# A modulated two-layer block on one core: the first modulation loaded and used in smaller parts, and some VectorE steps hung elsewhere

## The chip, the core and the metric

The kernel runs on one core of a Trainium2 chip. The engines of a core run side by side, each with its own queue of instructions that it takes in order: TensorE (PE in the profile, with its weight loads as PEld), VectorE (DVE), ScalarE (ACT), GpSimd (POOL) and SyncE (SP), whose queue here issues most of the transfers. The metric is the device time of one execution in microseconds. Before the change three runs took 585.10, 585.11 and 585.63 us, a median of 585.11.

## The reference, cut to what matters

The input x has 2 batches of 2048 tokens of width 512, everything in float32. A row of 512 numbers per batch (cond) gives six rows of modulation.

```
emb = silu(cond) @ ada_w + ada_b                      # ada_w is 512 x 3072
shift1, scale1, gate1, shift2, scale2, gate2 = split(emb, 6)
n  = ln(x) * (1 + scale1) + shift1
x  = x + gate1 * (gelu_erf(n @ w1 + b1) @ w2 + b2)     # 512 -> 512 -> 512
n  = ln(x) * (1 + scale2) + shift2
x  = x + gate2 * (gelu_tanh(n @ fw1 + fb1) @ fw2 + fb2) # 512 -> 1024 -> 512
```

`ln` takes mean and variance over the 512 columns of a token.

## The kernel before, in words

The 4096 tokens are cut into 8 blocks of 512 (`xs[i]`, i = 0 to 7; four blocks are one batch). A block is held as four slots c of 128 tokens. For each block the kernel makes n1 (the first normalised input, class `Norm`, which 1), hA (the first hidden layer, class `First`), the residual oA, n2 (`Norm`, which 2), hC (the second hidden layer, class `Second`) and the residual oC. The order of all this is written out by hand, block 0 and 1 first, then a loop over i = 1 to 7 in which the stages of neighbouring blocks are interleaved.

A matrix product is done with seven half-size products instead of eight, P1 to P7 in the code. Their operands are sums of quarters of the matrices: `sums_of_first` and `sums_of_second` (L350 in the profile) write them, for weights on POOL, for activations on DVE or POOL. A quarter of an activation is half of the columns of width (chunks k = 0, 1 or k = 2, 3 of 128) by half of the tokens of the block (slots c = 0, 1 or c = 2, 3). P1 of hA reads the first tokens of k = 0 and 1, P2 those of k = 2 and 3. Each product is accumulated in PSUM banks called y, x and v, read by DVE or ACT (L747, L757, L764, L767 for hidden layers, L802 for residuals), and the next product into the same bank waits for that read. The products of hC from block 1 on come from a table of 26 products, each of 128 x 256 twice (`products`, L1130 for the matmuls, L1147 for the reads on DVE, L1144 for those on ACT).

`hooks` is the means by which other work is put between products: `hook(hooks, places, ops)` hangs small pieces at named products, and each piece is issued just after the product and its read. An engine's own order follows from that, so a piece on DVE stands between two reads of products.

The start is this. SP issues the loads in order: x_0 in two halves, two slabs of ada_w (`load_ada`, 512 x 512 each: g = 0 for shift1, g = 1 for scale1), w1, x_1, the slab g = 2 (gate1), eight-descriptor pieces of ada_b for the gate, w2, b2, and so on. There are eight semaphores for transfers, used in turn by ACT's and SP's queues together, so the issue of a transfer waits for the one eight places before it. PE runs matmuls on a unit matrix (`warm`, tile `idle`) until data is there. The vectors cond, ada_b, b1 and fb1 come in on ACT's queue and are turned by PE (tile `rowsT`) into columns (`colsT`). `modulation(0, part)` makes 16 matmuls of 32 output rows over four chunks of the contraction (L276, tile `pada`), a transpose of 128 x 128 on DVE (L293) and an addition (L297). Block 0 is normalised on ACT and DVE (L627, L631), turned by PE (L656, 16 transposes, chunk by chunk over the four slots), and scaled and shifted by `modulate` on ACT (L676) and DVE (L678) from PSUM, one instruction of 128 x 512 for each k. Then hA_0 begins (`py_hA`, L496). Inside hA_0 stand the statistics of x_1 on ACT (L545, L556), the gate rows (L276, L305), the spread of the gate to all partitions (L312, `pgate`, which needs the 0/1 matrix `picks`), and the multiplication of w2 by the gate (`fold`, L398).

Three places further on matter here. In the residual of block 1 and the first group of hC_0 the eight row chunks of fw2 are multiplied by gate2, one DVE instruction of 128 x 512 each (`fold5`, L398). For the second batch the gates are folded again, and with them the biases: `gate_bias` loads b2 or fb2 and its `multiply` multiplies the row by the gate on DVE (L1030) and takes the first half from the second (`apart_row`, L479). For b2 this hangs at step 8 of the 26 products of hC_3 (`late_bias`), for fb2 at the last product of hA_5.

Of the kernel before, what the change touches and what calls it, by code (L numbers as in the profile page):

```python
# [36 lines left out]
F32 = mybir.dt.float32  # L37
# [103 lines left out]
def kernel(  # L141
# [65 lines left out]
    def load_ada(g):  # L207
        ada[g] = big_tile(f"ada_{g}")
        nc.sync.dma_start(
            out=ada[g], in_=ada_w[:, g * D : (g + 1) * D].rearrange("(k p) n -> p k n", p=P)  # L210
        )

    def load_w(name, w, t=None, eng=nc.sync):
        if t is None:
            t = const.tile([P, w.shape[0] // P, w.shape[1]], F32, tag=name, name=name)
        eng.dma_start(out=t, in_=w.rearrange("(k p) n -> p k n", p=P))
        return t
# [22 lines left out]
    ident = w2_t[:, :P]  # L240
    make_identity(nc, ident)
    load_x(0, 2)
    load_ada(0)
    load_ada(1)
    w1_sb = load_w("w1", w1)
    load_x(1)
    load_ada(2)

# [35 lines left out]
                )  # L284
        return pa

    def modulation(g0, part, pa=None):

        g = g0 + part
        if pa is None:  # L290
            pa = rows_of(g)
        turned = pa[:, P : 2 * P]
        nc.vector.transpose(turned, pa[:, :P])  # L293
# [3 lines left out]
        nc.vector.tensor_tensor(m, turned[:, :, :B], bias.unsqueeze(2).to_broadcast([P, KD, B]), ALU.add)  # L297
        mods[g0, part] = m
# [178 lines left out]
    def apart_row(row, eng):  # L477

        eng.tensor_tensor(row[:, D // 2 :], row[:, D // 2 :], row[:, : D // 2], ALU.subtract)  # L479
# [40 lines left out]
    class Norm:  # L520
# [57 lines left out]
        def rest(self, scratch=None):  # L578
# [11 lines left out]
            v.tensor_tensor(self.nmr, self.mv[:, :, 0], self.rstd, ALU.mult)  # L590
            v.tensor_scalar(self.nmr, self.nmr, -1.0, None, ALU.mult)

        def steps(self, scratch=None):
# [58 lines left out]
        def transpose(self, k, pt=None):  # L652
            if pt is None:
                pt = ps_t.tile([P, TB], F32, tag="t", name=f"pt{self.name}_{k}")
            for c in range(C):
                nc.tensor.matmul(  # L656
                    pt[:, c * P : (c + 1) * P],
                    self.xn[:, c, k * P : (k + 1) * P],
                    ident,
                    start=(c == 0),  # L660
                    stop=(c == C - 1),
                    is_transpose=True,
                    skip_group_check=True,
                )
            return pt

        def modulate(self, k, pt=None, eng=None):
# [3 lines left out]
            dst = self.nT.rearrange("p a (k c q) -> p a k c q", k=KD, c=C)[:, :, k]  # L671
            src = dst if pt is None else pt.rearrange("p (c a q) -> p a c q", c=C, a=C)
            if pt is None:
                dst = src = self.nT[:, :, k * P : (k + 1) * P]
            if eng is None:
                nc.scalar.activation(dst, src, AF.Identity, bias=shift, scale=scale)  # L676
            else:
                eng.tensor_scalar(dst, src, scale, shift, ALU.mult, ALU.add)  # L678

        def turned(self, on_dve=()):  # L680

            return [
                lambda k=k: self.modulate(k, self.transpose(k), nc.vector if k in on_dve else None)
                for k in range(KD)
            ]

        def moved(self, engs=(None,)):

# [337 lines left out]
    def gate_bias(g, b, row, name):  # L1026

        t = load_row(work.tile([P, D], F32, tag=f"gb{g}", name=name, bufs=1), row)
        def multiply():
            nc.vector.tensor_tensor(t, gate[g, b], t, ALU.mult)  # L1030
            apart_row(t, nc.vector)

        return t, multiply

# [182 lines left out]
    b1T = colsT[:, R_B1:R_FB1]  # L1217
    fb1T = colsT[:, R_FB1:ROWS]

    idle = ps_g.tile([P, C, P], F32, tag="v", name="idle")  # L1220
    def warm(count, blocks=2):
        for _ in range(count):
            nc.tensor.matmul(
# [10 lines left out]
    warm(1, 1)  # L1234

    run(n1[0].stats())
    nc.vector.tensor_copy(colsT, pt[:, :ROWS])


    nc.scalar.activation(  # L1240
# [2 lines left out]
        AF.Silu,  # L1243
    )

    for g in (1, 4):
        rows_g = colsT[:, R_ADA + g * KD : R_ADA + (g + 1) * KD]
        nc.vector.tensor_scalar(rows_g, rows_g, 1.0, None, ALU.add)

    picks = brows[:, 3].rearrange("p (m q) -> p m q", m=P // G)  # L1250
# [3 lines left out]
    n1[0].scales()  # L1254

    w1_ops, w1_sums, _ = weight_of_first("w1", w1_sb)
    run(w1_sums)
    modulation(0, 0)
    warm(3)
    for c in range(C):  # L1260
        n1[0].normal(c, nc.vector if c % 2 else None, on_pe=True)
    modulation(0, 1)
    pts = {}

    def transposed(k):
        pts[k] = n1[0].transpose(k, ps_g.tile([P, TB], F32, tag="yv"[k % 2], name=f"pt1_0_{k}"))

    for k in range(KD):
        transposed(k)
    for k in range(KD):  # L1270
        n1[0].modulate(k, pts[k], nc.vector if k % 2 else None)
# [159 lines left out]
    for i in range(1, NBLK):  # L1431
# [167 lines left out]
        hooks = {}  # L1599
        hook(hooks, ("P1",), [begin])  # L1600
        if refold5:
            hook(hooks, ("P4",), [multiply_5])
            hook(hooks, ("P5",) * 6 + ("P7", "P7", "P3"), folds)
        if refold2:
            def bias_2():
                take_gate(2, b)
                gb[2], multiply_2 = gate_bias(2, b, b2, f"gb2_{b}")
                return multiply_2
# [63 lines left out]
```

## Time and profile before

| | us |
|---|---|
| median of three runs | 585.11 |
| the profiled execution | 585.16 |
| its span in the profile | 583.3 |
| PE busy | 575.7 |
| DVE busy | 442.7 |
| POOL busy | 416.5 |
| ACT busy | 284.4 |

Between the span and the time of the profiled execution lie 1.86 us that no engine's rows show. The timeline view gives for each row the start and the length in us from the start of the span, the engine, the line, the operation, output and inputs, shapes and count; brackets at the end hold the idle time of the engine before the row and what ended it. The PE rows hold two passes per matmul instruction, so 4 instructions show as x8.

### The profile page before, as it was taken

How to read it: one execution, taken by the hardware profiler on the slowest of the kernel's cores; microseconds unless marked ns; L12 is line 12 of the kernel's file. 1: busy time of each engine (PE TensorE's matmuls, PEld its weight loads, DVE VectorE, ACT ScalarE, POOL GpSimd, SP SyncE). 2: the span in 40 equal slices, each digit the busy share in tenths (PEclk: the TensorE clock that was granted, in tenths of full speed). 3: DMA queues.
4: the chain of work that ended last, by engine and by line, in shares of the span. 5: the costliest groups of instructions: out<-in, count | busy, mean ns of one | idle time of the engine just before them, and what ended most of it. 6: DMA issues, size and time to landing. Idle time of an engine off the chain costs nothing.

```text
span 583.3 us, 9818 instructions
## 1 busy us (share of the span) xinstructions
PE 575.7 (99%) x3359; PEld 514.4 (88%) x3359; DVE 442.7 (76%) x893; ACT 284.4 (49%) x546; POOL 416.5 (71%) x446
## 2 busy tenths in 40 slices
PE   8999999999999999999999999999999999999997
PEld 4888888888899889998899988998888998899896
DVE  4877888896878576796967678986766487787676
ACT  2828357805652655545634588326664331732520
POOL 1575449999949788599968999998770593369351
PEclk9999999999999999999999999999999999999999
DMA  8977423302205303353033820243130330031002
GB/s 320 391 212 257 105 69 83 103 37 108 60 15 144 145 1 73 119 174 105 2 92 72 305 76 22 51 106 133 52 73 0 98 120 1 1 74 74 0 1 73
DMA packets 26014, 57.57 MB, mean 99 GB/s; under 512 B 4928, under 2 KB 5996, under 8 KB 24300
## 3 DMA queue, kind: packets, MB, share of 16 engines
q1 hardware_dynamic: 22240, 52.20, 28.3%
q10 hardware_dynamic: 3724, 4.75, 3.3%
q8 instruction: 27, 0.44, 0.3%
q14 instruction: 23, 0.19, 0.1%
HBM read 32.80 MB, written 8.40 MB: 71 GB/s over the span
## 4 chain that ended last, share of the span: by engine, by line
PE 88%; DVE 4%; DMA 2%; POOL 2%; ACT 1%; SPq 1%; issue 1%; ACTq 0%; DVEq 0%; POOLq 0%
PE px_hC L1130 10%; PE py_hA L496 8%; PE py_oC L904 8%; PE pv_hC L1130 8%; PE py_hC L1130 8%; PE pl_oC_P_y L952 8%; PE pl_oC_P_v L952 5%; PE pv_hA L496 4%; PE py_oA L839 4%; PE py_oA L496 3%; PE pl_oC_P_x L952 3%; PE py_oC L496 2%; PE py_hC L496 2%; PE px_hA L496 2%; PE pv_oC L952 2%; PE pl_oA_y L854 2%
## 5 line engine op out<-in xcount | busy, mean ns | idle before, releaser
L576 POOL TENSOR_TENSOR r<-ve,minus_half 128x4 f32<-128x4 f32 x16 | 16.6, 1039 | 71.7 <-DVE pl_oC_P_v L604 33.8
L676 ACT ACTIVATE nT<-nT,mod,mod 128x512 f32<-128x512 f32 x34 | 24.9, 804 | 67.8 <-DVE x L966 25.8
L1054 POOL TENSOR_TENSOR forms<-forms 128x256 f32<-128x256 f32 x56 | 42.5, 759 | 4.8 <-DVE forms L1050 1.3
L1130 PE MATMUL py_hC<-forms,fw 128*128 128x256 f32 x168 | 41.4, 381 | 0.4 <-DVE hClo L1147 0.4
L350 POOL TENSOR_TENSOR hSC<-hClo,hChi 128x512 f32<-128x512 f32 (+1 forms) x16 | 19.0, 1193 | 26.5 <-ACT hChi L1125 22.9
L1147 DVE TENSOR_TENSOR hClo<-hClo,py_hC 128x512 f32<-128x512 f32 x42 | 28.5, 683 | 11.1 <-ACT hClo L1144 8.7
L1130 PEld LDWEIGHTS py_hC<-forms,fw 128*128 128x128 f32 x168 | 31.6, 190 | 5.7 <-DVE hClo L1147 1.4
L533 DVE BATCH_NORM_STATS2 st<-x 128x6 f32<-128x512 f32 x48 | 32.4, 676 | 4.9 <-DMA x<-in_x_dram 4.9
L676 ACT ACTIVATE x<-x,mod,mod 128x512 f32<-128x512 f32 x24 | 17.6, 802 | 34.6 <-DMA x<-blocks 25.4
L627 ACT ACTIVATE nT<-x,nmr,rstd 128x512 f32<-128x512 f32 x36 | 26.8, 804 | 7.5 <-DVE nmr L612 4.9
L638 DVE STREAM_TRANSPOSE blocks<-nT 128x512 f32<-128x512 f32 x36 | 25.0, 704 | 5.9 <-ACT nT L627 5.9
L1147 DVE TENSOR_TENSOR hChi<-hChi,pv_hC 128x512 f32<-128x512 f32 x35 | 23.2, 680 | 8.0 <-PE pv_hC L1130 5.4
L1125 ACT ACTIVATE hClo<-hClo,colsT 128x256 f32<-128x256 f32 x56 | 25.3, 499 | 5.6 <-DVE hClo L1147 5.4
L1130 PE MATMUL px_hC<-forms,fw 128*128 128x256 f32 x112 | 27.6, 379 | 0.0
L966 DVE TENSOR_TENSOR x<-pl_oC_P_y,x 128x256 f32<-128x256 f32 (+1 forms) x66 | 24.6, 374 | 1.9 <-PE pl_oC_P_y L952 0.6
L1125 ACT ACTIVATE hChi<-hChi,colsT 128x256 f32<-128x256 f32 x56 | 25.1, 496 | 1.9 <-DVE hChi L1147 1.9
L1144 ACT ACTIVATE hClo<-px_hC 128x512 f32<-128x512 f32 x21 | 12.5, 596 | 27.6 <-PE px_hC L1130 19.3
L904 PE MATMUL py_oC<-fw_s,hSC 128*128 128x256 f32 x112 | 25.3, 379 | 0.0
L904 PE MATMUL py_oC<-fw,hClo 128*128 128x256 f32 x112 | 25.3, 379 | 0.0
L350 POOL TENSOR_TENSOR hClo<-hClo 128x512 f32<-128x512 f32 (+1 forms) x23 | 24.4, 1063 | 0.0
L1144 ACT ACTIVATE hChi<-py_hC 128x512 f32<-128x512 f32 x14 | 7.6, 594 | 34.4 <-PE py_hC L1130 25.5
L1130 PEld LDWEIGHTS px_hC<-forms,fw 128*128 128x128 f32 x112 | 21.3, 190 | 2.9
(403 smaller groups left out, 1850.8 us busy)
## 6 DMA issues: line engine op xcount, KB each, us to landing
x<-in_x_dram SPq DMA_DIRECT2D x13, 1024.0 KB
out_dram<-x SPq DMA_DIRECT2D x14, 512.0 KB
ada<-in_L_cond_ada_w_dram SPq DMA_DIRECT2D x6, 1024.0 KB
x<-blocks SPq DMA_DIRECT2D x96, 64.0 KB
nT<-blocks SPq DMA_DIRECT2D x88, 64.0 KB
fw<-in_L_cond_ff_w_dram SPq DMA_DIRECT2D x2, 2048.0 KB
nT<-blocks ACTq DMA_DIRECT2D x56, 64.0 KB
w<-in_L_cond_ssm_w_dram SPq DMA_DIRECT2D x3, 1024.0 KB
```

The lines of the kernel that those rows point to most:

```text
L350: eng.tensor_tensor(out[:, r], a[:, r], b[:, r], f)
L496: nc.tensor.matmul(ps[b][j * apart][:, j, :], lhs(p, j, k), rhs(p, j, k), start=(fresh and j * (not apart) == 0 and k == 0), stop=(p in (" ...
L533: nc.vector.bn_stats(st, xs[self.i][:, c, :])
L627: nc.scalar.activation(t, x_c, AF.Identity, bias=self.nmr[:, c : c + 1], scale=self.rstd[:, c : c + 1])
L638: nc.vector.transpose(self.bl[:, :, :, c, :].rearrange("p m k q -> p k m q"), self.nT[:, c, :].rearrange("p (k m q) -> p k m q", k=KD, m=C),)
L676: nc.scalar.activation(dst, src, AF.Identity, bias=shift, scale=scale)
L904: yield lambda j=j, k=k: nc.tensor.matmul(ps[BANK[p]][:, j, :], hops(p, j, k), wops[p][:, k, :], start=False, stop=(k == kdim - 1), skip_g ...
L952: nc.tensor.matmul(t[:, n, :], hops.leaves[p][f][:, k, :], leaf_wops[p][f][:, k, :], start=room not in started, stop=(f in ("P2", "P3", "P ...
L1054: eng.tensor_tensor(reg[d], reg[a], reg[b], ALU.add if f == "+" else ALU.subtract)
L1125: nc.scalar.activation(h, h, AF.Gelu_apprx_tanh, bias=fb1T[:, m : m + 1])
L1130: nc.tensor.matmul(ps[b][:, j, :], fa[ra][:, j * P : (j + 1) * P], fb[rb].rearrange("p a (c q) -> p c a q", q=Q), start=(fresh and j == 0) ...
L1147: nc.vector.tensor_tensor(dest(d), dest(d), ps[b], op)
```

## The change: what it does

- The slabs of shift1 and scale1 are loaded together by parts of the contraction: chunks k = 0 and 1 (1 MB), then k = 2, then k = 3 (0.5 MB each), in rows of 4 KB. w1 is loaded in two halves of its rows. SP so issues two more transfers ahead of x_1.
- `rows_01` makes the matmuls of both parts chunk by chunk into one PSUM tile, and `modulation_01` turns and adds both at once (128 x 256). Two of the three `warm` matmuls between them are gone.
- `colsT` is copied by ACT instead of DVE; `picks` is copied by POOL behind the sums of w1 instead of by DVE; `first_steps` needs one small DVE instruction fewer than `steps`.
- The 16 transposes of block 0 go slot by slot: slot 1 ahead of the matmuls of k = 3, slots 0, 3 and 2 behind them.
- `modulate` of block 0 has two instructions of 128 x 256 for each k, first tokens first.
- Of the eight `fold5` pieces the third moves from the last product of oA_1 to P6 of hC_0, and the later ones move so that two hang at P5.
- `gate_bias.multiply` becomes three instructions of 128 x 256, which leave the first product of the second half in the gate's PSUM tile; for b2 they hang at steps 5, 8 and 12 of hC_3 instead of both at 8; for fb2 they stay at the last product of hA_5.

```diff
-    load_ada(0)
-    load_ada(1)
-    w1_sb = load_w("w1", w1)
+    ada_01 = [big_tile(f"ada_{h}").rearrange("p (k g) n -> p k (g n)", g=2) for h in range(2)]
+    def load_ada_01(ks):
+        nc.sync.dma_start(
+            out=ada_01[ks[0] // 2][:, ks[0] % 2 : ks[-1] % 2 + 1],
+            in_=ada_w[ks[0] * P : (ks[-1] + 1) * P, : 2 * D].rearrange("(k p) n -> p k n", p=P),
+        )
+    load_ada_01((0, 1))
+    load_ada_01((2,))
+    load_ada_01((3,))
+    w1_sb = const.tile([P, KD, D], F32, tag="w1", name="w1")
+    load_half("w1", w1, w1_sb, 0)
+    load_half("w1", w1, w1_sb, 1)
...
+    def rows_01(pa, ks):
+        for k in ks:
+            w = ada_01[k // 2][:, k % 2].rearrange("p (g n m q) -> p g m n q", g=2, n=KD, q=G)
+            for g in range(2):
+                for m in range(P // G):
+                    nc.tensor.matmul(
+                        pa[m * G : (m + 1) * G, g * P : (g + 1) * P],
+                        silu[:, k, :],
+                        w[:, g, m],
...
+    def modulation_01(pa):
+        turned = pa[:, 2 * P : 4 * P]
+        nc.vector.transpose(turned, pa[:, : 2 * P])
+        turned = turned.rearrange("p (g n q) -> p g n q", g=2, n=KD)
+        m = const.tile([P, 2, KD, B], F32, tag="mod_0", name="mod_0")
+        bias = colsT[:, R_ADA : R_ADA + 2 * KD].rearrange("p (g n) -> p g n", g=2)
+        nc.vector.tensor_tensor(m, turned[:, :, :, :B], bias.unsqueeze(3).to_broadcast([P, 2, KD, B]), ALU.add)
...
+            else:
+                part = slice(h * C // 2, (h + 1) * C // 2)
+                dst = self.nT.rearrange("p a (k c q) -> p a k c q", k=KD, c=C)[:, :, k, part]
+                src = pt.rearrange("p (c a q) -> p a c q", c=C, a=C)[:, :, part]
...
         def multiply():
-            nc.vector.tensor_tensor(t, gate[g, b], t, ALU.mult)
-            apart_row(t, nc.vector)
+            pg, lo, hi = gate[g, b], slice(0, D // 2), slice(D // 2, D)
+            return [
+                lambda: nc.vector.tensor_tensor(t[:, lo], pg[:, lo], t[:, lo], ALU.mult),
+                lambda: nc.vector.tensor_tensor(pg[:, hi], pg[:, hi], t[:, hi], ALU.mult),
+                lambda: nc.vector.tensor_tensor(t[:, hi], pg[:, hi], t[:, lo], ALU.subtract),
+            ]
...
-    nc.vector.tensor_copy(colsT, pt[:, :ROWS])
+    n1[0].root()
+    nc.scalar.copy(colsT, pt[:, :ROWS])
...
+    n1[0].first_steps()
+    w1_ops, w1_sums, _ = weight_of_first("w1", w1_sb)
+    run(w1_sums)
+    pada_01 = ps_t.tile([P, D], F32, tag="t", name="pada_01")
+    rows_01(pada_01, (0, 1))
+    warm(1)
+    for c in range(C):
+        n1[0].normal(c, nc.vector if c % 2 else None, on_pe=True)
     for g in (1, 4):
...
-    modulation(0, 0)
-    warm(3)
-    for c in range(C):
-        n1[0].normal(c, nc.vector if c % 2 else None, on_pe=True)
-    modulation(0, 1)
...
+    rows_01(pada_01, (2,))
+    n1[0].transpose(1, pts, True)
+    rows_01(pada_01, (3,))
+    for c in (0, 3, 2):
+        n1[0].transpose(c, pts, False)
+    modulation_01(pada_01)
+    for h in range(2):
+        for k in range(KD):
+            n1[0].modulate(k, pts[k], nc.vector if k % 2 else None, h)
...
-    nc.vector.tensor_copy(
+    nc.gpsimd.tensor_copy(
         picks, ident.rearrange("p (m q) -> p m q", q=G)[:, :, :1].to_broadcast([P, P // G, P])
...
-    hook(hooks, ("P7", "P3", "P4"), fold5(0, 3))
+    hook(hooks, ("P7", "P3"), fold5(0, 2))
...
-    hook(hooks, ("P6", "P5", "P7", "P3", "P4"), fold5(3, 8))
+    hook(hooks, ("P6", "P5", "P5", "P7", "P3", "P4"), fold5(2, 8))
...
-            hook(hooks, (8,), late_bias)
+            hook(hooks, (5, 8, 12), late_bias)
...
-            hook(hooks, ("P4",), [multiply_5])
+            hook(hooks, ("P4",), multiply_5())
...
-            late_bias = [lambda: found["gb2"]()]
+            late_bias = [lambda n=n: found["gb2"][n]() for n in range(3)]
```

More of the change, by code (lines that the diff above doesn't have):

```diff
@@ L285, in rows_of, with modulation @@
         return pa
-    def modulation(g0, part, pa=None):
+    def rows_01(pa, ks):
[7 more added lines that the diff above has]
+                        w[:, g, m],
+                        start=(k == 0 and g == 0),
+                        stop=(k == KD - 1),
+                        tile_position=(0, m * G),
+                        skip_group_check=True,
+                    )
+    def modulation_01(pa):
[5 more added lines that the diff above has]
+        nc.vector.tensor_tensor(m, turned[:, :, :, :B], bias.unsqueeze(3).to_broadcast([P, 2, KD, B]), ALU.add)
+        for part in range(2):
+            mods[0, part] = m[:, part]
+    def modulation(g0, part, pa):
         g = g0 + part
-        if pa is None:
-            pa = rows_of(g)
         turned = pa[:, P : 2 * P]
@@ L591, in rest, with first_steps @@
             v.tensor_scalar(self.nmr, self.nmr, -1.0, None, ALU.mult)
+        def first_steps(self):
+            n, v = self.name, nc.vector
+            self.rstd, self.nmr = [small.tile([P, C], F32, tag=t, name=f"{t}{n}") for t in ("rstd", "nmr")]
+            room = ps_t.tile([P, D], F32, tag="t", name=f"small{n}")
+            a, b = room[:, :C], room[:, C : 2 * C]
+            v.tensor_scalar(a, self.mv[:, :, 1], EPS, None, ALU.add)
+            v.tensor_tensor(b, self.r, a, ALU.mult)
+            v.scalar_tensor_tensor(b, b, -0.5, self.r, ALU.mult, ALU.mult)
+            v.scalar_tensor_tensor(self.rstd, b, 1.5, self.r, ALU.add, ALU.mult)
+            v.scalar_tensor_tensor(self.nmr, self.mv[:, :, 0], -1.0, self.rstd, ALU.mult, ALU.mult)
         def steps(self, scratch=None):
@@ L650, in move, with transpose @@
                     )
-        def transpose(self, k, pt=None):
-            if pt is None:
-                pt = ps_t.tile([P, TB], F32, tag="t", name=f"pt{self.name}_{k}")
-            for c in range(C):
+        def transpose(self, c, pts, first):
+            for k in range(KD):
                 nc.tensor.matmul(
-                    pt[:, c * P : (c + 1) * P],
+                    pts[k][:, c * P : (c + 1) * P],
                     self.xn[:, c, k * P : (k + 1) * P],
                     ident,
-                    start=(c == 0),
-                    stop=(c == C - 1),
+                    start=first,
+                    stop=True,
                     is_transpose=True,
@@ L678, in modulate @@
                 eng.tensor_scalar(dst, src, scale, shift, ALU.mult, ALU.add)
[L680 to L685, printed above, removed]
         def moved(self, engs=(None,)):
@@ L1248 @@
         nc.vector.tensor_scalar(rows_g, rows_g, 1.0, None, ALU.add)
+    pts = [ps_g.tile([P, TB], F32, tag=t, name=f"pt1_0_{k}") for k, t in enumerate("yvxv")]
+    rows_01(pada_01, (2,))
[5 more added lines that the diff above has]
+    for h in range(2):
+        for k in range(KD):
+            n1[0].modulate(k, pts[k], nc.vector if k % 2 else None, h)
     picks = brows[:, 3].rearrange("p (m q) -> p m q", m=P // G)
-    nc.vector.tensor_copy(
+    nc.gpsimd.tensor_copy(
         picks, ident.rearrange("p (m q) -> p m q", q=G)[:, :, :1].to_broadcast([P, P // G, P])
     )
-    n1[0].scales()
-    w1_ops, w1_sums, _ = weight_of_first("w1", w1_sb)
-    run(w1_sums)
-    modulation(0, 0)
-    warm(3)
-    for c in range(C):
-        n1[0].normal(c, nc.vector if c % 2 else None, on_pe=True)
-    modulation(0, 1)
[L1263 to L1271, printed above, removed]
     n1_sums = n1[0].summed(nc.vector)
```

9 lines of the change are left out of this document (3 added, 6 removed).

## The prediction

> **What bounds the kernel now.** I read the busy times, then the chain of work that ended last, the timeline around the places that the diff touches, and busy time by stretches.
>
> ```profile
> span 583.3 us, 9818 instructions
> PE 575.7 (99%) x3359; PEld 514.4 (88%) x3359; DVE 442.7 (76%) x893; ACT 284.4 (49%) x546; POOL 416.5 (71%) x446
> ```
> ```profile
> 14.70:73.40 58.70, 58.30 (x379) 49.11 (x377) 46.70 (x90) 33.55 (x69) 32.74 (x29) 1.00 0.73 239
> ```
>
> The second fence is one stretch: its length, then busy time of PE, weight loads, DVE, ACT and POOL, the granted clock, the DMA share and GB/s. PE is the bound: from 14.70 on it is idle for 0.4 us in 58.7. The change removes no product, so it can gain only by starting the products earlier, before 14.8 us, or by closing the few holes in PE's stream. The chain gives the pace of that stream and the length of a tiny transfer:
>
> ```profile
> 16.73 1.73 PE px_hA L496 x8
> ...
> 62.74 1.98 DMA gates<-w_t
> ```
>
> Eight passes of a product take 1.73 us, one 0.216.
>
> **The start.** The timeline of before:
>
> ```profile
> 11.96 0.39 SPq L216 DMA_DIRECT2D w<-in_L_cond_ssm_w_dram  x1
> ...
> 11.99 1.08 PE L276 MATMUL pada<-ada,w_t 128*32 128x128 f32 x32
> ...
> 13.00 1.97 PE L656 MATMUL pt<-w_t,blocks 128*128 128x128 f32 x16
> ...
> 13.14 0.33 DVE L293 STREAM_TRANSPOSE pada<-pada 128x128 f32<-128x128 f32 x1 [0.79 <-PE pada L276]
> ...
> 13.51 0.17 DVE L297 TENSOR_TENSOR mod<-pada,colsT 128x8 f32<-128x8 f32 x1
> ...
> 13.76 1.59 ACT L676 ACTIVATE nT<-pt,mod,mod 128x512 f32<-128x512 f32 x2 [1.20 <-PE pt L656]
> ...
> 14.70 1.27 POOL L350 TENSOR_TENSOR w_s<-w 128x512 f32<-128x512 f32 x1 [4.56 <-DMA w<-in_L_cond_ssm_w_dram]
> ...
> 14.81 1.92 PE L496 MATMUL py_hA<-nT,w 128*128 128x256 f32 x8
> ...
> 17.25 0.63 ACT L545 ACTIVATE unread<-x 128x512 f32<-128x512 f32 x1 [1.90 <-DMA x<-in_x_dram]
> ...
> 23.05 0.17 DVE L575 TENSOR_SCALAR ve<-mv 128x4 f32<-128x4 f32 x1 [0.88 <-ACT unread L556]
> ...
> 23.73 0.28 DVE L305 TENSOR_TENSOR w_t<-pada,fw_t 128x128 f32<-128x128 f32 x1
> ...
> 24.47 1.08 PEld L312 LDWEIGHTS pgate<-w_t,fw_t 128*128 128x128 f32 x8
> ...
> 29.10 0.57 ACT L468 COPY py_oA<-gb 128x512 f32<-128x512 f32 x1
> ...
> 30.02 1.70 PEld L496 LDWEIGHTS py_oA<-w,forms 128*128 128x128 f32 x8
> ...
> 30.44 0.84 ACT L771 ACTIVATE forms<-py_hA,colsT 128x256 f32<-128x256 f32 x2 [0.21 <-PE py_hA L496]
> ```
>
> The second slab lands at 11.95 (SP issues the next load at 11.96, having waited for it); its matmuls, the 16 transposes and the first `modulate` (0.80) follow. Then hA_0 starts at 14.81, just behind w1, which lands at about 14.65 (POOL's first sum of it starts at 14.70).
>
> **Part 1, the first product.** The same bytes stand in the same queue, so k = 3 should land at 11.95 too. Its 8 matmuls are half of a group of 16: 0.54, to 12.5. Four transposes already lie under the wait for it; 12 remain (12/16 of 1.97 = 1.48, to 14.0). Each `modulate` waits for the last transpose of its k, so k = 0 is free after nine: 12.5 + 9 x 0.123 = 13.6. The joint transpose of 128 x 256 is not in the trace; between 0.33 (half as wide) and 0.66, it ends with the 0.17 addition at 13.0 to 13.4, hidden behind the PE transposes. A `modulate` of 128 x 256 from PSUM costs half of 0.84 = 0.42 by the last row, at worst the whole 0.80. Taking 0.42, which is its shape, k = 0 is done at 14.05 on ACT and k = 1 at 14.2 on DVE; hA_0 starts at 14.2, 0.6 earlier; at worst 0.3 earlier, at best right behind the transposes, 0.8. The first half of w1 lands midway between 11.95 and 14.65, at 13.3; the second is wanted by P2 at 14.2 + 1.73 = 15.9. The sums of w1 on POOL still wait for both halves, so end as before. The earlier normalisation (`colsT` off DVE, one small step less) is worth nothing by itself: its cover is the wait for k = 3, and without it four or twelve transposes would come later. The `picks` copy on POOL follows the four sums of w1, which from 14.70 on, each at the 1.27 of the first or up to a third more, end by about 21.5; `pgate` wants it at 24, so a copy of as many elements as that row hides. `warm` shortened leaves PE waiting for k = 2, nothing else queued.
>
> **Part 2, what survives of it.** Little of x_1's work moves: ACT's statistics start at its landing (17.25), DVE's `ve` waits for the last of them (23.05), and in DVE's queue behind `ve` stand a read of P6 and the gate rows (23.73 + 0.28 = 24.01). `pgate` on PE loads at 24.47, 0.46 after them. So of 0.6 at most about 0.45 passes. A little later ACT, busy from x_1's normalisation on, ends the seed of py_oA at 29.67 where PE loads at 30.02: about 0.35 passes there. I take 0.4; bounds 0 and, if x_1 should land a little earlier too, 0.8. From there to 73 us DVE's folds, the transfers of the turned blocks and PE follow one another, and carry it on.
>
> SP issues x_1 later, as it now waits for the small b1 transfer with the slab for gate1, the gate's bias rows and w2 queued behind. The transfers are busy without a hole there, so this costs nothing while 2 MB are still ahead of it:
>
> ```profile
> 9.30:11.94 2.64, 2.57 (x38) 1.90 (x38) 1.63 (x9) 0.90 (x2) 0.83 (x1) 1.00 1.05 387
> 11.94:14.64 2.70, 2.65 (x47) 2.45 (x48) 1.42 (x4) 1.47 (x3) 0.00 (x0) 1.00 1.09 416
> 14.64:17.16 2.52, 2.52 (x15) 2.26 (x13) 2.35 (x4) 0.71 (x1) 2.38 (x2) 1.00 0.98 391
> ```
>
> Whole transfers of 1 MB follow each other at 387 to 416 GB/s with the share at 1: no fixed cost shows between them. The Trainium skill, page "DMA: Bandwidth & Descriptors", section "Rules for kernel authors", speaks against the cut: it wants at least 1 MiB per transfer. Its section on the anatomy of a transfer issued from GpSimd gives a fixed part of about 2.0 us; by that, two more transfers would put x_1 4.0 us later and the sum at about 587.4 (an estimate). The three rows speak for the other sum.
>
> **Part 3, the fold moved out of oA_1.**
>
> ```profile
> 71.11 1.89 PE L496 MATMUL px_hC<-nT,fw 128*128 128x256 f32 x8
> ...
> 72.01 0.68 DVE L398 TENSOR_TENSOR fw<-fw,pgate 128x512 f32<-128x512 f32 x1
> ...
> 72.13 1.27 POOL L350 TENSOR_TENSOR nT<-nT 128x512 f32<-128x512 f32 x1
> ...
> 72.60 0.68 DVE L747 TENSOR_TENSOR hClo<-py_hC,colsT 128x512 f32<-128x512 f32 x1
> ...
> 73.43 1.96 PE L496 MATMUL py_hC<-nS,fw_s 128*128 128x256 f32 x8 [0.43 <-POOL nT L350]
> ...
> 75.23 1.89 PE L496 MATMUL pv_hC<-nS,fw_s 128*128 128x256 f32 x8
> ...
> 78.96 0.69 DVE L764 TENSOR_TENSOR hChi<-py_hC,hChi 128x512 f32<-128x512 f32 x1
> ...
> 80.41 1.89 PE L496 MATMUL py_hC<-nS,fw 128*128 128x256 f32 x8
> ```
>
> From 71.11 to 75.23 are 4.12 us for 16 passes (3.46): a hole of 0.66. The profile names POOL's `nT`, but P6 reads nS, which POOL had finished when it began `nT` at 72.13. The read of P1 from the same bank ends at 73.28, queued behind the fold. Without the fold it ends 0.6 earlier, at 72.7, against the end of the products before at 72.84; I take 0.58 of the hole, bounds 0 (if POOL does own it) and 0.66. Next late is the read of P7: it moves forward with its product, but one fold (0.6) now stands ahead of it, so it still starts near 79.0 and ends at 79.7; P4, 0.6 earlier, wants it at 79.8. It just fits; if not, up to 0.1 comes back.
>
> **Part 4, gate times b2.**
>
> ```profile
> 276.59 0.69 DVE L1147 TENSOR_TENSOR hClo<-hClo,px_hC 128x512 f32<-128x512 f32 x1 [0.67 <-PE px_hC L1130]
> ...
> 277.19 0.68 DVE L1030 TENSOR_TENSOR gb<-pgate,gb 128x512 f32<-128x512 f32 x1
> ...
> 277.91 1.17 DVE L479 TENSOR_TENSOR gb<-gb 128x256 f32<-128x256 f32 x1
> ...
> 279.84 1.03 PE L1130 MATMUL py_hC<-forms,fw 128*128 128x256 f32 x4
> ...
> 280.55 0.68 DVE L1147 TENSOR_TENSOR hClo<-hClo,py_hC 128x512 f32<-128x512 f32 x1
> ...
> 281.28 1.13 PE L1130 MATMUL py_hC<-forms,fw 128*128 128x256 f32 x4 [0.42 <-DVE hClo L1147]
> ...
> 282.25 1.03 PE L1130 MATMUL px_hC<-forms,fw 128*128 128x256 f32 x4
> ...
> 339.13 0.42 DVE L479 TENSOR_TENSOR gb<-gb 128x256 f32<-128x256 f32 x1
> ...
> 340.75 1.28 DVE L1147 TENSOR_TENSOR hChi<-hChi,pv_hC 128x512 f32<-128x512 f32 x2 [1.19 <-PE px_hC L1130]
> ```
>
> 279.84 to 282.25 is 2.41 for 8 passes (1.73): a hole of 0.68, because the read of py_hC ends at 281.23. Of the 1.8 us of bias work ahead of it, one instruction of about 0.42 goes into the idle 0.67 before 276.59, one stays, one goes behind the read. So 1.4 us less stand ahead, and the read would be over near 279.9, before the product of 279.84 ends at 280.7. The hole closes: 0.68; bounds 0.4 (if the new places make another read late) and 0.68. For fb2, three times 0.42 replace 0.68 + 0.42; the 0.2 more lies in the idle 1.19 before 340.75. Uncovered it would cost 0.2.
>
> **The sum.** 0.4 + 0.58 + 0.68 = 1.66. The profiled execution took 585.16 (the span of 583.3 and 1.86 around it, taken as unchanged), 0.05 above the median; 585.16 - 1.66 = 583.5.
>
> **The rivals.** *Slower.* Two more transfers ahead of x_1 cost a tiny transfer's 1.98 each: x_1 lands 3.96 later, the gate rows come at 27.97, and past the 0.46 of room PE waits 3.5. With parts 3 and 4 (1.26) still gained: 585.16 + 3.5 - 1.26 = 587.4. It decides once x_1 is later by more than 1.72. Against it: the even landings above. *Only one hole closes.* POOL owns the hole at 73, and x_1's chain swallows the start: 0.68 alone, 584.5, within what counts as no change (0.2% or 1.17 us, about what a measurement can tell). For it: the releaser that the profile names. *More.* hA_0 at its best with x_1 landing earlier: 0.8 + 0.66 + 0.68, 583.0 or somewhat below.
>
> **How the numbers follow.** Forecast 0.52 and more 0.14, together faster by over 0.2%: 0.66. One hole only, with all that ends in between: 0.17. Slower 0.17. The forecast's own range, from the bounds of its three terms, is 582.9 to 583.9. For 8 in 10 I take 582.3, below "more", to 586.3, through the middle case and towards the slower one.
>
> **What would show it.** hA_0 starting near 14.2; ACT's first `unread` still near 17.2; `pgate` loading near 24.1; no hole before P6 of hC_0's first group and none in hC_3; PE's busy share up, its work unchanged. Wrong it would be if x_1 lands past 17.6, if the hole at 73 stays with the fold gone, or if new holes open behind the moved folds.

## The result and the profile after

The changed kernel takes 584.16 us (median of 14 executions, 583.43 to 584.54) against 585.2 for the kernel before beside it: a ratio of 0.9978 with a 95% interval of 0.997 to 0.9986, so 0.8 to 1.8 us faster. The forecast of 583.5 had the direction; the gain is 1.0 by the medians and 1.3 by the ratio, where 1.66 was forecast. The profiled execution took 584.29 us. Its page begins:

```profile
span 582.5 us, 9821 instructions
...
PE 575.2 (99%) x3355; PEld 513.4 (88%) x3355; DVE 442.5 (76%) x892; ACT 284.9 (49%) x549; POOL 417.0 (72%) x447
```

PE's work is the same and the span is 0.8 shorter. The timeline of the start has these rows, which answer to those shown of before:

```profile
10.13 0.70 PE L1267 MATMUL idle<-w_t 128*128 128x256 f32 x2
10.76 0.65 PE L304 MATMUL pada<-ada,w_t 128*32 128x128 f32 x16
11.33 0.66 PE L702 MATMUL pt<-w_t,blocks 128*128 128x128 f32 x4
11.92 0.65 PE L304 MATMUL pada<-ada,w_t 128*32 128x128 f32 x16
...
12.63 0.47 DVE L317 STREAM_TRANSPOSE pada<-pada 128x256 f32<-128x256 f32 x1 [1.20 <-PE pada L304]
...
13.73 1.93 ACT L723 ACTIVATE nT<-pt,mod 128x256 f32<-128x256 f32 x4 [1.94 <-PE pt L702]
...
14.35 1.99 PE L532 MATMUL py_hA<-nT,w 128*128 128x256 f32 x8 [0.33 <-ACT nT L723]
...
18.34 0.63 ACT L581 ACTIVATE unread<-x 128x512 f32<-128x512 f32 x1 [2.69 <-DMA x<-in_x_dram]
...
24.14 0.17 DVE L611 TENSOR_SCALAR ve<-mv 128x4 f32<-128x4 f32 x1 [2.16 <-ACT unread L592]
...
24.82 0.28 DVE L341 TENSOR_TENSOR w_t<-pada,fw_t 128x128 f32<-128x128 f32 x1
...
25.24 1.13 PE L348 MATMUL pgate<-w_t,fw_t 128*128 128x128 f32 x8 [0.79 <-DVE small L652]
...
30.87 0.43 PE L532 MATMUL py_oA<-w,forms 128*128 128x256 f32 x1
```

The row of before that answers to the last one, and those of three products further on that are needed below:

```profile
30.24 1.89 PE L496 MATMUL py_oA<-w,forms 128*128 128x256 f32 x8
...
76.96 1.89 PE L496 MATMUL py_hC<-nT,fw 128*128 128x256 f32 x8
...
349.28 2.15 PE L1130 MATMUL py_hC<-forms,fw 128*128 128x256 f32 x8
...
351.27 1.03 PE L1130 MATMUL px_hC<-forms,fw 128*128 128x256 f32 x4
```

hA_0 starts 0.46 earlier (14.35 for 14.81), but ACT reads x_1 1.09 later (18.34 for 17.25), the gate rows follow 1.09 later (24.82 for 23.73), PE stands idle for 0.79 ahead of `pgate`, and oA_0 starts at 30.87 in place of 30.24. The start cost 0.63 in this trace instead of gaining 0.4. The same view of after further on:

```profile
71.84 1.89 PE L532 MATMUL px_hC<-nT,fw 128*128 128x256 f32 x8
...
73.72 1.97 PE L532 MATMUL py_hC<-nS,fw_s 128*128 128x256 f32 x8
75.53 1.89 PE L532 MATMUL pv_hC<-nS,fw_s 128*128 128x256 f32 x8
...
280.29 1.89 PE L1174 MATMUL py_hC<-forms,fw 128*128 128x256 f32 x8
...
282.02 1.03 PE L1174 MATMUL px_hC<-forms,fw 128*128 128x256 f32 x4
...
349.02 2.01 PE L1174 MATMUL py_hC<-forms,fw 128*128 128x256 f32 x8
...
350.86 1.03 PE L1174 MATMUL px_hC<-forms,fw 128*128 128x256 f32 x4
```

From 71.84 to 75.53 are 3.69 us for 16 passes, where before it was 4.12. From 280.29 to 282.02 are 1.73 for eight passes, where before it was 2.41: that hole is gone. Two smaller ones, which the forecast did not price, shrink. The eight passes from 349.02 take 1.84 to the next product, where before the like stretch (349.28 to 351.27) took 1.99. Near 390 a stretch of four groups of products takes 2.68 (389.13 to 391.81), where before it took 3.04 (389.54 to 392.58).

From here on a hole is given by the distance from one start to the next, less the 0.216 per pass of the stream; the idle time in a row's brackets is shorter by what PE counts as busy (at 352 below, 0.33 for a hole of 0.50).

How far the products of after lie behind those of before shows where the time went:

```
start of, us                              after    before   difference
oA_0                                      30.87     30.24     +0.63
px of hC_0's first group                  71.84     71.11     +0.73
py of hC_3 ahead of the hole of Part 4   280.29    279.84     +0.45
px behind that hole                      282.02    282.25     -0.23
px behind the hole at 349                350.86    351.27     -0.41
(end of the span)                        582.5     583.3      -0.8
```

The start loses 0.73 by the time of hC_0. Part 3 gains 0.28, Part 4 0.68, the hole at 349 gains 0.18, and from there to the end 0.39 are gained, nearly all of it near 390.

### The profile page after: what moved, and what is told of

Its sections match the earlier page's. It is cut to its first block, busy times and chain, and to the rows that moved or that the text cites. A ratio compares the mean times of both kernels' runs of the same rounds, so it can differ in the third digit from the quotient of the medians.

```text
span 582.5 us, 9821 instructions
## 1 busy us (share of the span) xinstructions
PE 575.2 (99%) x3355; PEld 513.4 (88%) x3355; DVE 442.5 (76%) x892; ACT 284.9 (49%) x549; POOL 417.0 (72%) x447
## 4 chain that ended last, share of the span: by engine, by line
PE 93%; DMA 3%; DVE 2%; ACT 1%; issue 1%; ACTq 0%; SPq 0%; DVEq 0%
PE px_hC L1174 10%; PE py_hA L532 9%; PE py_hC L1174 8%; PE py_oC L944 8%; PE pv_hC L1174 8%; PE pl_oC_P_y L992 8%; PE py_oA L532 5%; PE pl_oC_P_v L992 5%; PE pv_hA L532 4%; PE py_oA L879 4%; PE pl_oC_P_x L992 3%; PE py_hC L532 2%; PE pv_oA L532 2%; PE py_oC L532 2%; PE px_hA L532 2%; DMA x<-in_x_dram 2%
## 5 line engine op out<-in xcount | busy, mean ns | idle before, releaser
L723 ACT ACTIVATE nT<-nT,mod,mod 128x512 f32<-128x512 f32 x32 | 23.4, 803 | 56.0 <-DMA nT<-blocks 32.7
L723 ACT ACTIVATE x<-x,mod 128x512 f32<-128x512 f32 x24 | 17.6, 802 | 34.9 <-DMA x<-blocks 25.8
```

## Why x_1 comes late

The first theory is called fetch in the expectations: PE's instructions come in packets of 16 KB over the same DMA engines as the data, each packet is asked for after a fixed count of PE instructions, and a packet that meets x_1 holds up the sixteenth of x_1 on its engine. It came from two things in the trace of after, which records the landing of each of the sixteen parts into which a transfer of 1 MB is split, and the packets of each queue. (These times stand in the trace itself; the views do not list them one by one.)

```
landings of x_1, us        fifteen parts       the last part
before                     16.16 to 17.05      17.15
after                      15.84 to 16.78      18.24
16 KB instruction packet   before 18.65        after 15.93
```

In the changed kernel fifteen parts land earlier than before, and one is 1.46 behind. What lies there shows in the view of the DMA queues of after, cut to 15.9 to 17.05 us (packets, MB, share of 16 engines):

```profile
q1 hardware_dynamic: 210, 0.43, 100.9%
q8 instruction: 1, 0.02, 5.9%
```

There is one instruction packet: 5.9% of 16 engines in 1.15 us is 1.09 us of one engine. 127 of x_1's 128 packets of 8 KB start by 15.98, the last at 17.00, when that packet is over. Before, the packet lay at 18.65, behind x_1. The Trainium skill, page "DMA: Bandwidth & Descriptors", section "Queues, rings and completion order", says that each engine takes turns between the queues packet by packet, and the section "Why a DMA increments its semaphore by 16 and not by 1" that the engines finish independently and all of them must be in; the sixteen landings here agree with both. That the packet is TensorE's is inferred: the run has 27 packets of 16 KB, PE has by far the most instructions, and in the trace of before one packet comes for 254 PE instructions on average.

The rival is called *transfers*: the two transfers more ahead of x_1, and its later issue, put it back.

## The experiments

Each result gives the median in us, its ratio to the kernel before on the same chip with the 95% interval, and the difference from the kernel before by that ratio.

**Parts 3 and 4 alone** (holes_only; the start as before):

```diff
+    hook(hooks, ("P7", "P3"), fold5(0, 2))                               # Part 3, with fold5(2, 8) on hC_0
+            hook(hooks, (5, 8, 12), late_bias)                           # Part 4, with the split gate_bias
```

> The kernel before with only Parts 3 and 4 (the fold moved out of oA_1, gate times b2 as three instructions at steps 5, 8 and 12), the start as before. If the start of the changed kernel gained 0.4 as forecast, this is slower than the changed kernel by 0.4. If the start cost the 0.63 that oA_0 starts later by in its profile (30.24 to 30.87), this is faster than the changed kernel by about 0.6: the holes at 71 (0.45), 279.8 (0.58), 349 (0.26) and 389 to 392 (0.3) gone, 1.3 to 1.6 below the kernel before, 583.5 to 583.9.

The median is 584.23; 0.9982 (0.9973 to 0.9991), 1.05 faster. That is about the level of the changed kernel, and neither of the two levels expected: on top of these parts the start as changed adds little. The trace has no hole at 73 and 280 any more, but 0.30 ahead of P7 (76.53), 0.50 at 352 and 0.95 at 390; its execution, 585.17, is the slowest of the eleven.

**The start alone** (start_only; Parts 3 and 4 undone):

> The changed kernel with Parts 3 and 4 undone: only the start is changed. Forecast of the prediction's Part 2: 0.4 faster than before, 584.8. By the profile of the changed kernel, with x_1 landing at 18.3 in place of 17.2: slower by 0.6, about 585.8. The 16 KB instruction packet of the queue q8 should again lie in the landing of x_1, near 16, if it is what holds x_1 up.

The median is 584.91; 0.9991 (0.9982 to 1.0): at most 1.05 faster, at least nothing. The profiled execution shows the same loss as that of after: the packet at 16.04, x_1 read at 18.46, oA_0 at 31.00. Its own time of 585.52 lies above the median, so that trace is not the commonest case.

**Two fillers taken out of the changed kernel** (fewer_fillers):

```diff
     warm(1, C)
-    warm(1, 1)
...
     rows_01(pada_01, (0, 1))
-    warm(1)
```

> The changed kernel without two of its filler products (one of 128x128 behind the transposed rows, one of 128x256 behind the first rows of pada): four matmuls and four weight loads fewer on PE, no transfer changed. Theory fetch: PE asks for its next 16 KB of instructions after a fixed count of them, and that packet (1.09 us, at 15.93) holds one DMA engine and with it the last sixteenth of x_1. With 8 instructions fewer ahead it is asked for some 0.9 later, behind x_1: x_1 lands at 16.8 in place of 18.3, ve starts near 22.6, the hole ahead of pgate (1.05) closes, about 1.0 faster than the changed kernel: 583.1. Theory transfers (the two more transfers and the later issue put x_1 back): x_1 lands at 18.3 again and the time is that of the changed kernel, 584.2, or above it if PE's idle start costs clock.

The median is 583.15; 0.9966 (0.9954 to 0.9979), 2.0 faster, as the theory fetch had it. The profiled execution took 584.26, the slowest of five, but its span of 581.3 is that of the other four (581.3 to 581.5): what it took longer lies outside the span. All the transfers of the change are still there, so the rival transfers is out as the cause of a late x_1. The timeline:

```profile
9.20 1.84 PE L304 MATMUL pada<-ada,w_t 128*32 128x128 f32 x48 [0.95 <-DMA ada<-in_L_cond_ada_w_dram]
...
11.70 0.65 PE L304 MATMUL pada<-ada,w_t 128*32 128x128 f32 x16
...
14.13 1.99 PE L532 MATMUL py_hA<-nT,w 128*128 128x256 f32 x8 [0.33 <-ACT nT L723]
...
16.94 0.63 ACT L581 ACTIVATE unread<-x 128x512 f32<-128x512 f32 x1 [1.50 <-DMA x<-in_x_dram]
...
29.78 1.46 PE L532 MATMUL py_oA<-w,forms 128*128 128x256 f32 x6
```

x_1 is read 1.40 earlier than in after, and oA_0 starts 1.09 earlier. But hA_0 too starts 0.22 earlier: the rows of k = 3 begin at 11.70, not 11.92. So two things differ from after, and this run alone can't tell them apart.

**The reverse, on the kernel before** (more_fillers): the fillers are cut finer, into more instructions with the same columns in all.

```diff
-    warm(1, C)
+    warm(4, 1)
...
-    warm(3)
+    warm(6, 1)
```

> The kernel before with its fillers cut finer (one of 128x512 as four of 128x128, three of 128x256 as six of 128x128): twelve matmuls and twelve weight loads more on PE, the same columns or fewer, no transfer changed. Theory fetch: the 16 KB packet, at 18.65 in the kernel before, comes about 2.6 earlier, near 16.0, and falls into x_1, which lands near 18.2 in place of 17.2; pgate loads about 0.6 later and the time is 0.4 to 0.7 above the kernel before. Theory transfers: x_1 lands at 17.2 and the time is the same.

The median is 585.82; 1.0008 (0.9999 to 1.0017), 0.5 slower by the ratio, but the interval still holds no change at all. The trace did what the theory said. The queue view from 15.9 to 17.05, and the timeline:

```profile
q8 instruction: 1, 0.02, 6.0%
```
```profile
18.50 0.63 ACT L545 ACTIVATE unread<-x 128x512 f32<-128x512 f32 x1 [3.22 <-PE px_hA L496]
...
25.31 1.16 PE L312 MATMUL pgate<-w_t,fw_t 128*128 128x128 f32 x8 [0.53 <-DVE w_t L305]
...
30.98 0.48 PE L496 MATMUL py_oA<-w,forms 128*128 128x256 f32 x1
```

The packet moved from 18.65 to 16.26, x_1's last part to 18.39 (the one before it lands at 17.10), `pgate` on PE 0.63 (24.68 before) and oA_0 0.74 later, with no transfer changed. (The profile names a matmul as what ACT waited for; that had long been done, and the landing ends just before.) In the three traces in which the packet lies on x_1 (after, start_only and this one), oA_0 starts 0.63 to 0.76 later than before; only here is the start otherwise that of before (hA_0 at 14.73).

**The changed kernel once more** (after_again), for a second trace:

> The changed kernel once more, for a second trace of it. Theory fetch: the instruction packet lies near 15.9 again and x_1's last share lands 1.2 to 1.5 behind its other fifteen, near 18.3. If x_1 lands near 16.8 here, the packet meets x_1 in some executions only, and that would be part of the spread of its times. Time as before, 583.9 to 584.4.

The median is 584.15; 0.9982 (0.9974 to 0.9991). The time is the same and the trace is not:

```profile
8.37 0.23 PE L1276 MATMUL rowsT<-w_t,fw_t 44*128 44x44 f32 x1 [1.56 <-DMA fw_t<-in_L_cond_ff_b_dram]
8.53 1.35 PE L1267 MATMUL idle<-w_t 128*128 128x512 f32 x4
9.81 1.08 PE L304 MATMUL pada<-ada,w_t 128*32 128x128 f32 x32
10.82 0.70 PE L1267 MATMUL idle<-w_t 128*128 128x256 f32 x2
11.45 0.64 PE L304 MATMUL pada<-ada,w_t 128*32 128x128 f32 x16
...
12.61 0.64 PE L304 MATMUL pada<-ada,w_t 128*32 128x128 f32 x16
...
15.04 2.00 PE L532 MATMUL py_hA<-nT,w 128*128 128x256 f32 x8 [0.33 <-ACT nT L723]
...
17.39 0.63 ACT L581 ACTIVATE unread<-x 128x512 f32<-128x512 f32 x1 [1.04 <-DMA x<-in_x_dram]
...
30.78 0.59 PE L532 MATMUL py_oA<-w,forms 128*128 128x256 f32 x2
```

The packet came at 21.81 and x_1 was read at 17.39, 0.14 later than before the change. Here the last small row (fb1) landed late, `rowsT` ran at 8.37 in place of 7.34, and the rows of k = 0 and 1 began at 9.81, in the first trace at 9.12. hA_0 started at 15.04, 0.23 later than before the change, and oA_0 again at 30.78. So there is a second way to lose the start, and it has two shares. The last part of every transfer from k = 0 and 1 to x_1 lands about 0.5 behind the other fifteen (9.51 for 9.00, 12.12 for 11.58, 17.29 for 16.78), with no instruction packet before 21.81; what held it up was not found. The other share is the fillers', which keep PE from the rows of k = 3 after these have landed:

```
rows of k = 3, us    last part landed   begun on PE
after                     11.58            11.92
start_only                11.69            12.04
after_again               12.12            12.61
w1_whole                  11.62            12.11
fewer_fillers             11.65            11.70
fewer_again               11.62            11.66
start_fewer               11.65            11.70
short_fillers             11.63            11.67
no_late_fillers           11.61            11.65
```

With the two fillers (the first four) the rows wait 0.34 to 0.49 beyond the landing; without them, or with short ones (the last five), it is 0.04 or 0.05. The runs not yet named follow below.

**The start alone, without the two fillers** (start_fewer):

> The start alone (Parts 3 and 4 undone) with the two fillers taken out, so that the instruction packet falls behind x_1: what the start is worth when nothing holds x_1 up. The prediction's Part 2 with x_1 a little earlier: oA_0 starts near 29.8 in place of 30.24, 0.4 to 0.5 faster than before, and 0.6 to 1.1 faster than the start with its fillers. If the start is worth nothing even so, it is the time of the kernel before.

The median is 584.17; 0.9987 (0.9978 to 0.9995), 0.76 faster; oA_0 starts at 29.78. So 0.46 arrives at oA_0 when nothing stands in the start's way; in this trace the hole at 73 grows by 0.15 and the holes near 390 close too. The expected 0.6 to 1.1 over the start with its fillers is not shown: the two ratios, 0.9991 and 0.9987, differ by 0.24 us, well within their intervals.

**Two more runs on the theory: the gain again, and its cause.** The first kernel (fewer_again) is the one without the two fillers once more. In the second (short_fillers) the two fillers stay as instructions but have 16 columns.

```diff
-    warm(1, 1)
+    warm(1, 1, 16)
...
-    warm(1)
+    warm(1, 1, 16)
```

> The changed kernel without the two fillers once more. Theory fetch: x_1 lands near 16.9 again, oA_0 starts near 29.8, 583.1 to 583.3, and the times lie closer together than those of the changed kernel, since the instruction packet no longer meets x_1 in some executions and not in others. If the first result was a chance of its executions, about 584.2.

> The changed kernel with the same two fillers cut to 16 columns: as many instructions on PE as in the changed kernel, PE as idle there as without the fillers. Theory fetch: the count of instructions decides, so the packet comes near 16 and x_1's last share near 18.3, and the time is that of the changed kernel, 584.0 to 584.3. If PE's idle time at the start (and not the count) made the gain, 583.1 to 583.3.

The medians are 583.29, 0.9967 (0.9954 to 0.9979), without the fillers and 583.18, 0.9966 (0.9953 to 0.9978), with short ones. The gain repeats, and it does not need fewer instructions: here the theory fetch, in the form that the count decides, fails. The timeline with short fillers:

```profile
10.17 0.39 PE L1267 MATMUL idle<-w_t 128*128 128x16 f32 x2
10.50 0.64 PE L304 MATMUL pada<-ada,w_t 128*32 128x128 f32 x16
...
11.67 0.64 PE L304 MATMUL pada<-ada,w_t 128*32 128x128 f32 x16
...
14.10 1.99 PE L532 MATMUL py_hA<-nT,w 128*128 128x256 f32 x8 [0.33 <-ACT nT L723]
...
16.92 0.63 ACT L581 ACTIVATE unread<-x 128x512 f32<-128x512 f32 x1 [1.51 <-DMA x<-in_x_dram]
...
29.72 1.46 PE L532 MATMUL py_oA<-w,forms 128*128 128x256 f32 x6
```

The packet lay at 16.60, behind x_1, although PE was ahead of the changed kernel by 0.25 with as many instructions. Counted in PE's own instructions its place is not fixed either: the matmuls and other PE instructions that had started before it are 212 in after, 213 in fewer_fillers, 223 here, 242 in before, 243 with the fillers cut finer, 261 in after_again and 333 in w1_whole.

**w1 in one transfer (w1_whole), and no filler at all behind the transposed rows (no_late_fillers):**

```diff
-    load_half("w1", w1, w1_sb, 0)
-    load_half("w1", w1, w1_sb, 1)
+    w1_sb = load_w("w1", w1)                # the first kernel
...
-    warm(1, C)                              # the second, beside the two above
```

> The changed kernel with w1 in one transfer of 1 MB in place of two halves. Theory transfers (each transfer more ahead of x_1 costs): x_1 lands 0.5 or more earlier, 583.5 or less. Theory fetch: no transfer costs anything by its number; the packet still falls near 16, x_1 lands near 18.3 where it meets it, and the time is within 0.3 of the changed kernel, 584.0 to 584.4 (hA_0 starts at 14.35, just behind the whole of w1 at 14.3).

> The changed kernel without any filler behind the transposed rows (a third one, of 128x512, gone too): six matmuls and six weight loads fewer than in the changed kernel. Theory fetch: once the packet is behind x_1 nothing more is to be had, 583.1 to 583.4, the packet near 17. If the fillers carry PE's speed, the rows of pada and the transposes get slower (0.54 for 16 of 128x32, 0.12 for a transpose) and it is slower than with one of them.

With w1 in one transfer the median is 584.51, 0.9984 (0.9975 to 0.9993): a transfer fewer is not faster. The packet, expected near 16, came at 23.22. Without any late filler it is 583.15, 0.997 (0.9959 to 0.9981): the third filler is worth nothing that can be told. Without it PE idles for 2.30 us ahead of 9.16, and 16 rows of pada still take 0.65 and 16 passes of transposes 1.53 and 0.66, at a granted clock of 1.00. The Trainium skill, page "TensorE: Matmul & The Clock Gate", section "Part 1: The HAM clock gate (the "warmup" mystery)", puts the loss of speed behind an idle window of about 3.4 us; a gap of 2.30 without loss agrees.

All traces with the changed start, in us:

```
                     hA_0    packet   x_1 read  pgate loads  oA_0
after                14.35   15.93    18.34     25.21        30.87
start_only           14.47   16.04    18.46     25.34        31.00
after_again          15.04   21.81    17.39     25.01        30.78
w1_whole             14.62   23.22    17.12     24.32        30.45
fewer_fillers        14.13   16.50    16.94     23.86        29.78
fewer_again          14.09   16.98    16.91     23.82        29.75
start_fewer          14.13   16.67    16.97     23.86        29.78
short_fillers        14.10   16.60    16.92     23.84        29.72
no_late_fillers      14.09   16.57    16.91     23.82        29.78
```

With the fillers the start varies by 0.7 at hA_0 and 0.55 at oA_0; without them, or with short ones, it stays within 0.06. Two things are shown. A packet on x_1 puts its last part 1.3 to 1.5 behind the others (after, start_only and the finer fillers). Long fillers hold the rows of k = 3 by 0.3 to 0.45 more than short or no ones. The packet is not needed for the loss: in after_again and w1_whole it is off x_1, and oA_0 still starts 0.7 to 1.1 later than without the fillers, in after_again with the late sixteenth parts as well, in w1_whole with 0.29 of waiting for a slab at 27.61. Open is what sets the place of the packet, whether shorter fillers also keep it off x_1 or five traces fell so by chance, and how much of the last 1.0 us belongs to each.

**Part 3 alone (fold_only), Part 4 alone (bias_only):**

> The kernel before with Part 3 alone. Forecast 0.58: no hole before P6 of hC_0's first group (73.43 comes at 72.84). In the run of Parts 3 and 4 together the product after the next, P7, waited 0.30 in its place (76.53), so 0.25 to 0.58 faster than before. If POOL owns the hole, nothing.

With Part 3 alone the median is 584.82; 0.9997 (0.9988 to 1.0006): nothing that can be told. The timeline, and below it the row of before for the same read on ACT:

```profile
72.84 1.95 PE L496 MATMUL py_hC<-nS,fw_s 128*128 128x256 f32 x8
...
73.93 1.28 ACT L758 ACT_TABLE_LOAD   x1
...
75.76 0.82 ACT L745 ACTIVATE hClo<-py_hC,colsT 128x256 f32<-128x256 f32 x2
...
76.73 1.97 PE L496 MATMUL py_hC<-nT,fw 128*128 128x256 f32 x8 [0.21 <-ACT hClo L745]
```
```profile
75.74 0.82 ACT L745 ACTIVATE hClo<-py_hC,colsT 128x256 f32<-128x256 f32 x2
```

P6 starts at 72.84, 0.59 earlier than before and without a hole, so POOL's `nT`, which was not moved, did not own it. But P7 then waits for ACT's read of P6's result, which ends at 76.58 here and ended at 76.56 before. P7 starts 0.23 earlier than before (76.96), and two products later 0.15 is left (80.26 for 80.41).

> The kernel before with Part 4 alone. Forecast 0.68 (0.4 to 0.68): no hole at 279.8 and none new at the steps 5 and 12; the holes at 73, 349 and 389 as before.

With Part 4 alone the median is 584.43; 0.999 (0.9981 to 0.9999), 0.59 faster. The hole at 279.8 is gone. In this trace PE idles for 0.71 ahead of P6 at 73.62, where before it was 0.43, and a hole of 0.50 stands at 352, where before there was one of 0.26 at 349:

```profile
350.34 0.17 DVE L608 TENSOR_TENSOR small<-r,small 128x4 f32<-128x4 f32 x1 [1.22 <-POOL r L576]
...
351.97 0.69 DVE L1151 TENSOR_TENSOR hClo<-hClo,py_hC 128x512 f32<-128x512 f32 x1 [0.39 <-ACT hClo L1148]
...
352.71 1.56 PE L1134 MATMUL py_hC<-forms,fw 128*128 128x256 f32 x6 [0.33 <-DVE hClo L1151]
```

DVE waits 1.22 for POOL's `r` in a small step of the normalisation, and reads of products queue behind it. In the trace of after that wait is not there. How large the hole at 349 is differs between traces (0.11 in after and fewer_fillers, 0.14 in after_again, 0.26 in before and fewer_again), and what sets it was not found.

## Why the prediction was right, and where it was wrong

The forecast was right in the direction and in Part 4; the size came about in part by luck. The start, worth 0.4 in the sum, lost instead, and holes that stood in no term made up for most of that. The first trace even shows one of the forecast's own signs of being wrong: x_1's last part lands at 18.24, past 17.6.

- *Part 1, hA_0 at 14.2.* Nearly: 14.35, and 15.04 in the second trace. Two errors met. k = 3 landed at 11.58 and not at 11.95, which by the forecast's own sum would have put hA_0 at 13.8. The step that failed, "`warm` shortened leaves PE waiting for k = 2, nothing else queued", gave that back: the remaining filler kept PE until 10.76, and the rows of k = 3 began at 11.92. With 16 columns the rows of k = 2 start at 10.50 and those of k = 3 at 11.67, and hA_0 at 14.10. The second trace lost further by sixteenth parts that landed 0.5 late, which the forecast did not price. Two sizes were short as well: the rows of k = 3 took 0.65 for 0.54, and half a `modulate` 0.48 for 0.42 (1.93 for four). The joint transpose (0.47, between 0.33 and 0.66) came as forecast.
- *Part 2, 0.4 with bounds 0 and 0.8.* This term was wrong by 1.0 in both traces of the changed kernel: oA_0 starts 0.54 and 0.63 later, below the lower bound. "Little of x_1's work moves" fell: in the first trace x_1 came 1.09 later. The bound excluded a loss for one cause only, the number of transfers, and on that it was right. Fifteen parts of x_1 land at 16.78, before the 17.15 of the kernel before, and w1 in one transfer gains nothing. The Trainium skill's rule of at least 1 MiB per transfer (page "DMA: Bandwidth & Descriptors", section "Rules for kernel authors"), weighed there, is not borne out for transfers that queue behind one another: the two halves of w1 land within 2.70 (11.58 to 14.28), the whole of it before within 2.68 (11.95 to 14.63). With the start freed, 0.46 arrives at oA_0, where 0.4 was forecast.
- *Part 3, 0.58.* At P6 0.59 came, as forecast; behind it the term was mis-sized: 0.23 at P7, 0.15 two products later, and no measurable gain alone. In the trace of after 0.28 is left. The step that failed is "Next late is the read of P7 ... up to 0.1 comes back". Next late was ACT's read of P6's result, behind x_2's normalisation and a table load of 1.28. Before, it ended 0.40 ahead of P7, and here P7 follows it by 0.15, so about 0.25 of room was all there was. The forecast weighed DVE alone. That DVE's read, and not POOL, held P6 was right.
- *Part 4, 0.68.* In the trace of after the whole 0.68 comes, and alone the part measures 0.59 (0.06 to 1.1).
- *Not in the sum:* the holes at 349 and near 390. With them the sum of the trace of after is +0.73 (start) - 0.28 (Part 3) - 0.68 (Part 4) - 0.18 - 0.39 = -0.80, the change of the span. They made good most of what the start lost.
- *The range.* The bounds of the three terms add up to gains of 0.4 to 2.14, which is 583.0 to 584.8 and not the 582.9 to 583.9 given as the forecast's own range. The measured 584.16 lies above the range as given, within the bounds as they add up, and within the range of 8 in 10.
- *The rivals.* "Slower" named the right place, x_1, and the wrong price: not 3.96 from two transfers, but 1.1 from an instruction packet, short of the 1.72 from which it would have decided. "Only one hole closes" had x_1's chain swallow the start, as it did, but lost the hole at 73, most of which closed in that trace. "More" needs the start that the fillers withheld: 583.15 to 583.29 without them.

The best kernel run is the changed one without the two fillers, or with short ones: 0.9966 (0.9954 to 0.9979) against 0.9978 (0.997 to 0.9986) of the changed one; the two intervals still overlap a little.

## What to carry to other kernels

A filler that keeps an engine busy while it waits is work in that engine's queue: set its end against the landings that it should only bridge, the early ones too, and try the kernel without it. A transfer is as late as its last part, so a landing that moves while the rate does not is looked up part by part, with the instruction queue beside it. And when a hole on PE is closed by making one reader earlier, ask which reader on the *other* engines is late next, ACT's table loads among them.

## What was not expected of the hardware

A 16 KB instruction packet takes 1.09 us of one DMA engine in the middle of saturated loads, and the last sixteenth of the transfer that it meets lands 1.3 to 1.5 us behind the rest; the loads behind it keep the lag (in the trace of before the slab of gate1 and then w2, each with its last part some 1.2 behind the others: 21.00 for 19.85, 23.72 for 22.51). Its place is not fixed by the program: in two traces of the same kernel it came at 15.93 and 21.81. A sixteenth of every load can also lag by about 0.5 with no such packet near (after_again, 9.51 for 9.00 to 17.29 for 16.78).
